# A two-layer graph network on one core: preparation steps divided, edge counts moved beside the keys, the phases left beside the same groups

## The chip, the cores and the metric

The kernel runs on one core of a Trainium2 chip. The metric is the device time of one execution in microseconds; the time before is the median of three runs. The profile is of one execution.

The engines are TensorE (PE in the profile, PEld for its weight loads), VectorE (DVE), ScalarE (ACT), GpSimd (POOL) and SyncE (SP), which issues the DMAs. Each runs its own queue in order; semaphores tie them together.

## The reference

For each of 32 graphs with 512 nodes and 128 features:

```python
# layer 0
adj = adj + eye(N);  degree = adj.sum(axis=2);  d = degree ** -0.5   (0 where infinite)
x = layernorm(x + (d[:, :, None] * adj * d[:, None, :]) @ (x @ weight) + bias)
# layer 1
pre = (x @ W1[:D])[:, None, :, :] + (x @ W1[D:])[:, :, None, :] + b1      # every pair (i, j)
msg = gelu(layernorm(pre) * g1 + be1)
agg = einsum('bijo,bij->bio', msg, adjacency)
updated = layernorm(concat([x, agg]) @ W2 + b2) * g2 + be2
out = layernorm(x + updated)
```

About one in sixteen of the entries of `adj` is not zero, and a message counts only where the entry isn't.

## The kernel before

The kernel makes messages for the edges alone. A graph's 512 nodes are C = 4 blocks of P = 128, so the adjacency is 16 blocks of 128 x 128. For each node and block, `lists` finds the first 8 edges (VectorE's max and index of a key that ranks them), `more` finds 16 more (match, replace, max, index: lines 455 to 458), and `shared` packs what is left over into 2 more slots per block. The first 8 slots, one slot for the diagonal blocks' ninth edge and the 2 shared ones make the list `order` of 41 groups a graph: 8 x 4 + 1 + 2 x 4.

The main loop runs over 32 graphs and their 41 groups. In the iteration of group k, counted within its graph:

- `pairs` (lines 724, 725, and 720 for the shared slots) issues TensorE's products of group k into one of 3 PSUM tiles;
- `pass_on` issues the aggregate (L772, TensorE) of group k-3, the sums (L734, VectorE, which release the PSUM tile) and the weights (L749, GpSimd, 4 buffers) of group k-1, and the messages (L763, ScalarE, four activations) of group k-2;
- `advance(todo)` runs one step of `finish`, the tail of the graph before: it starts in iteration 2 of the next graph;
- `prepare` runs steps of the preparation phases of graphs to come.

Ahead of both, `fetch` issues the index loads, the one-hot comparison (L687, VectorE), its transposing DMA and the row loads of the slots that begin 5 and 3 groups later.

A phase is a Python generator, and a step is what it issues up to its next `yield`. The list `plan` gives each phase a number of steps and a range of iterations, relative to the graph that it prepares. The steps are spread evenly:

```python
while gen[1] < n_steps * (g + 1 - n0) // (n1 - n0):
```

So a phase with more steps than iterations runs two of them in some iterations. With 41 groups a graph, `layer0` (range -41 to -19) lies beside the iterations 0 to 21 of the graph before, `lists` beside 22 to 32, `more` beside 31 to 40 of the graph before and 0 to 7 of its own, `shared` beside 8 to 27 of its own. Within an iteration the order is: `finish`, `layer0`, `lists`, `parts`, `factors`, `more`, `shared`.

The instructions of ScalarE, GpSimd and VectorE stay in the order in which Python issues them (`tc.manual_schedule`). TensorE's and SyncE's order is made by the framework's scheduler.

Names and lines that matter here, in `layer0`: `a_nat` (the adjacency as loaded), `pa` (its transposed blocks in PSUM, L249), `copied` with `deg` (L260, ScalarE, row sums), `a_t` (L261, ScalarE's copy out of PSUM), `mask` (L263, VectorE, one instruction over all four blocks), the chain of small GpSimd instructions from the degrees to `dinv` (lines 277 to 287), `xb` (L289, GpSimd), the edge counts (L293, ScalarE, four activations that sum rows of the mask), `s` and `own_s` (L297, L302, ScalarE), `xb` plus `own_s` (L306, GpSimd), `pconv` (L311, TensorE), `y` (L318, VectorE), the norm (statistics L194 and L196 on VectorE, `ve`, `rstd`, `shift` on GpSimd in lines 199, 187, 204, 205, result L208 on ScalarE), `x1t` (L328), `pat` and `pct` (L333, L335), and the keys (L361, L362 on VectorE after L365 on TensorE). In `shared`: `over`, `count`, `here`, `counts` (lines 469 to 479, VectorE), `last`, `most` and `missed` (L493 to L501), the places (L502, L505, GpSimd), `ended` (L512, sixteen VectorE comparisons), `pj` and `sj` (L526 TensorE, L522 VectorE, eight each), `pl` and `sent` (L537 TensorE, L533 ScalarE, sixteen each). In `finish`: `pu` (L637, L638, TensorE), `u` (L641, VectorE), two norms with three additions and products of GpSimd between them (lines 645 to 649). `bank` hands out 4 PSUM banks in turn; a new user of a bank waits for the readers of the one before.

Of the kernel before, what the change touches and what calls it, by code (L numbers as in the profile page):

```python
# [8 lines left out]
F32 = mybir.dt.float32  # L9
BF16 = mybir.dt.bfloat16  # L10
I32 = mybir.dt.int32
U32 = mybir.dt.uint32
AF = mybir.ActivationFunctionType
ALU = mybir.AluOpType
# [4 lines left out]
P = 128  # L19
# [8 lines left out]
def bcast(ap, n):  # L28

    return ap.unsqueeze(1).to_broadcast([ap.shape[0], n, ap.shape[-1]])  # L30
# [16 lines left out]
def sparse_path(ctx, tc, x, adj, w0, b0, w1, b1, g1, be1, w2, b2, g2, be2, out, most):  # L47
# [21 lines left out]
    nc = tc.nc  # L69
    B, N, D = x.shape  # L70
    C = N // P
# [3 lines left out]
    node = ctx.enter_context(tc.tile_pool(name="node", bufs=1))  # L75
    small = ctx.enter_context(tc.tile_pool(name="small", bufs=2))
# [66 lines left out]
    rows = {}  # L143
# [69 lines left out]
    def bank(key):  # L213
        return ps.tile([P, 512], F32, tag="ps", name=key)

    def transposed(src, key):

        pt = bank(f"pt_{key}")
        for c in range(C):
            nc.tensor.transpose(pt[:, c * P : (c + 1) * P], src[:, c, :], ident)  # L220
        return pt
# [3 lines left out]
    def pause(n):  # L225

        for _ in range(n):
            yield

    def layer0(b):  # L230

        st = state[b] = {}
        xs = node.tile([P, C, D], F32, tag="xs", name=f"xs_{b}")
# [5 lines left out]
        a_t = big.tile([P, C, C, WIDE], F32, tag="a_t", name=f"a_t_{b}", bufs=2)  # L239
        st["a_t"] = a_t  # L240
        edges = small.tile([P, C], F32, tag="edges", name=f"edges_{b}")
        st["edges"] = edges
        deg = small.tile([P, C], F32, tag="deg", name=f"deg_{b}")
        mask = big.tile([P, C, N], BF16, tag="mask", name=f"mask_{b}")
        px = transposed(xs, f"x_{b}")
        for mc in range(C):
            pt = bank(f"pa_{b}_{mc}")
            for c in range(C):
                nc.tensor.transpose(  # L249
                    pt[:, c * P : (c + 1) * P], a_nat[:, c, mc * P : (mc + 1) * P], ident  # L250
                )
            if mc == 2:
                psup = bank(f"psup_{b}")
                for c in range(C):
                    nc.tensor.matmul(
                        psup[:, c * P : (c + 1) * P], x_t[:, c * P : (c + 1) * P], w0_sb, start=True, stop=True
                    )
            yield
            copied = small.tile([P, N], BF16, tag="copied", name=f"copied_{b}_{mc}", bufs=1)
            nc.scalar.activation(copied, a_nat[:, mc, :], AF.Copy, accum_out=deg[:, mc : mc + 1])  # L260
            nc.scalar.copy(a_t[:, mc, :, :P], pt.rearrange("p (c i) -> p c i", i=P))  # L261
            if mc == C - 1:
                nc.vector.tensor_scalar(  # L263
                    mask.rearrange("p q (c i) -> p (q c) i", i=P),
                    a_t.rearrange("p q c w -> p (q c) w")[:, :, :P],
                    0.0,
                    1.0,
                    ALU.is_equal,
                    ALU.subtract,
                )  # L270
            if mc == 0:
                x_t = node.tile([P, N], F32, tag="t0", name=f"x_t_{b}")
                nc.scalar.copy(x_t, px)
        yield from pause(2)

        deg1 = small.tile([P, C], F32, tag="deg1", name=f"deg1_{b}")
        nc.gpsimd.tensor_scalar(deg1, deg, 1.0, None, ALU.add)
# [6 lines left out]
        dinv = small.tile([P, C], F32, tag="dinv", name=f"dinv_{b}")  # L284
        nc.gpsimd.tensor_sub(dinv, rdeg, none)
        dinv2 = small.tile([P, C], F32, tag="dinv2", name=f"dinv2_{b}", bufs=1)
        nc.gpsimd.tensor_tensor(dinv2, dinv, dinv, ALU.mult)
        xb = node.tile([P, C, D], F32, tag="t2", name=f"xb_{b}")
        nc.gpsimd.tensor_tensor(xb, xs, bcast(rows["b0"], C), ALU.add)  # L289

        for q in range(C):
            copied = small.tile([P, N], BF16, tag="copied", name=f"counted_{b}_{q}", bufs=1)
            nc.scalar.activation(copied, mask[:, q, :], AF.Copy, accum_out=edges[:, q : q + 1])  # L293

        s = node.tile([P, C, D], F32, tag="t1", name=f"s_{b}")
        for c in range(C):
# [10 lines left out]
        pt = bank(f"pconv_{b}")  # L307
        for c in range(C):
# [4 lines left out]
                )  # L313
            if c % 2:
                yield
        y = node.tile([P, C, D], F32, tag="t3", name=f"y_{b}")
        for c in range(C):
            nc.vector.scalar_tensor_tensor(  # L318
                y[:, c, :], pt[:, c * P : (c + 1) * P], dinv[:, c : c + 1], xb[:, c, :], ALU.mult, ALU.add
            )  # L320
        x1 = node.tile([P, C, D], F32, tag="x1", name=f"x1_{b}", bufs=3)
        yield from layernorm(y, x1, f"l0_{b}")
        st["x1"] = x1
# [1 line left out]
        pt = transposed(x1, f"x1_{b}")  # L325
# [31 lines left out]
        key = big.tile([P, C, N], F32, tag="key", name=f"key_{b}")  # L357
        for q in range(C + 1):
            if q:
                here = key[:, q - 1, :]  # L360
                nc.vector.scalar_tensor_tensor(here, pt, a_sum[:, q - 1 : q], c_sum, ALU.add, ALU.add)  # L361
                nc.vector.scalar_tensor_tensor(here, here, -TINY, mask[:, q - 1, :], ALU.min, ALU.mult)  # L362
            if q < C:
                pt = bank(f"pv_{b}_{q}")
                nc.tensor.matmul(pt, at2[:, q * P : (q + 1) * P], ct, start=True, stop=True)  # L365
            yield
# [94 lines left out]
    def shared(b):  # L461
# [7 lines left out]
        nc.vector.scalar_tensor_tensor(over, var, 0.0, sharing, ALU.is_gt, ALU.mult)  # L469
        count = small.tile([P, C * C], F32, tag="count", name=f"count_{b}", bufs=1)  # L470
        nc.vector.tensor_reduce(count, over, AX.X, ALU.add)

        here = small.tile([P, C * C, SLOTS], F32, tag="here", name=f"here_{b}", bufs=1)
        nc.vector.tensor_scalar(here, st["top"], 0.0, None, ALU.is_gt)
# [11 lines left out]
        pt = bank(f"po_{b}")  # L486
# [32 lines left out]
        pt = None  # L519
        for k in range(len(chunks) + 1):  # L520
            if k:
                nc.vector.tensor_scalar(sj_f[:, chunks[k - 1]], pt, node_p, None, ALU.is_equal)  # L522
            if k < len(chunks):
                pt = bank(f"pj_{b}_{k}")
# [6 lines left out]
        for n in range(C * C + 1):  # L531
            if n:
                nc.scalar.copy(sent[:, n - 1], pt[:, : SHARED * WIDE].rearrange("p (k w) -> p k w", w=WIDE))  # L533
            if n < C * C:
                pt = bank(f"pl_{b}_{n}")
                for k in range(SHARED):
                    nc.tensor.matmul(  # L537
                        pt[:, k * WIDE : (k + 1) * WIDE],
                        sj[:, n, k * P : (k + 1) * P],
                        at[:, n, :],  # L540
                        start=True,
                        stop=True,
                    )
            if n % 2:
                yield
        yield from pause(3)

        n_r = SHARED * C * C
        chosen = big.tile([P, 2, SHARED, C * C, MORE], F32, tag="mask", name=f"chosen_{b}")
# [22 lines left out]
        pt = bank(f"pidx_s_{b}")  # L572
# [18 lines left out]
        pt = bank(f"psd_s_{b}")  # L591
# [38 lines left out]
    def finish(b):  # L630

        st = state.pop(b)
        aggt = st["aggt"]
        pt = bank(f"pu_{b}")
        for c in range(C):
            o, here = pt[:, c * P : (c + 1) * P], slice(c * P, (c + 1) * P)
            nc.tensor.matmul(o, st["x1t"][:, here], w2_sb[:, 0, :], start=True, stop=False)  # L637
            nc.tensor.matmul(o, aggt[:, here], w2_sb[:, 1, :], start=False, stop=True)  # L638
        yield
        u = node.tile([P, C, D], F32, tag="f0", name=f"u_{b}")  # L640
        nc.vector.tensor_tensor(u, pt.rearrange("p (c d) -> p c d", d=D), bcast(rows["b2"], C), ALU.add)  # L641
        yield
        un = node.tile([P, C, D], F32, tag="f1", name=f"un_{b}")
        yield from layernorm(u, un, f"l1_{b}")
        nc.gpsimd.tensor_tensor(un, un, bcast(rows["g2"], C), ALU.mult)
        yield
        nc.gpsimd.tensor_tensor(un, un, bcast(rows["be2"], C), ALU.add)
        yield
        nc.gpsimd.tensor_tensor(un, un, st["x1"], ALU.add)
        yield  # L650
        o_sb = node.tile([P, C, D], F32, tag="f0", name=f"o_sb_{b}")
        yield from layernorm(un, o_sb, f"l2_{b}")
        yield
        nc.sync.dma_start(out[b].rearrange("(c p) d -> p c d", p=P), o_sb)
# [111 lines left out]
    def aggregate(b, t, q, m, sw):  # L766
        st = state[b]
        begin, end = (t, q) == order[0], (t, q) == order[-1]
        if begin:
            st["agg"] = ps_g.tile([P, C, P], F32, tag="agg", name=f"agg_{b}")  # L770
        for c in range(C):
            nc.tensor.matmul(  # L772
                st["agg"][:, c, :],
                m[:, c, :],
                sw[:, c, :],
                start=(begin and c == 0),
                stop=(end and c == C - 1),
            )
        if end:
            st["aggt"] = node.tile([P, N], F32, tag="f1", name=f"aggt_{b}")  # L780
            nc.scalar.copy(st["aggt"], st["agg"].rearrange("p c i -> p (c i)"))
            todo.append(finish(b))

    def advance(gens, steps=1):
# [12 lines left out]

    n_groups = len(order)
    plan = [
        (layer0, 26, -n_groups, -19),  # L800
        (lists, 21, -19, -8),
        (parts, 7, -19, -10),
        (factors, 7, -8, -3),
        (more, 33, -10, 8),
        (shared, 45, 8, 28),
    ]
    running = {}

# [260 lines left out]
def kernel(  # L1069
# [32 lines left out]
    with ExitStack() as inner:  # L1102
        sparse_path(inner, tc, *args, most)
# [42 lines left out]
```

## Time and profile before

| what | value |
|---|---|
| median of 3 runs | 4013.91 us (4012.98 to 4014.3) |
| profiled execution, its own time | 4011.64 us |
| its span, first to last instruction | 4009.9 us |
| mean granted TensorE clock | 0.985 |
| busy: TensorE, VectorE, ScalarE, GpSimd | 94%, 81%, 70%, 55% of the span |
| VectorE's whole mask (L263) | 32 x 1.218 us |
| ScalarE's counts (L293) | 128 x 0.626 us, and 128 x 0.186 us for reading the sums |
| VectorE's `ended` (L512) | 512 x 0.337 us |

A line of a group or of the timeline names the line of the kernel, the engine, the instruction, what it writes and reads, and the shapes; in the timeline the first two numbers are start and duration in us, and what stands in brackets is how long the engine stood idle before it and what ended that. Instructions of one engine overlap a little at their ends, so what one costs its queue is read from its start to the start of the next.

### The profile page before, as it was taken

To read this page: it belongs to the slowest core of one execution; us is meant where nothing else is said; L and a number is where in the kernel's file an instruction comes from. 1 tells how busy PE (TensorE), PEld (TensorE's weight loads), DVE (VectorE), ACT (ScalarE), POOL (GpSimd) and SP (SyncE) were. 2 spreads that over 40 slices of the span, in tenths; PEclk is the share of its full clock that TensorE was granted. 3 is DMA by queue.
4 is the path that set the end of the run, shared out by engine and by line. 5 is a ranking of instruction groups with operands and counts; after the bars stand their busy time and mean duration, and the time that the engine had idled before them with its cause. 6 is when DMAs were issued, how large, how long until landed. Compare 5 with 4: busy or idle time off the path is not lost. (4 is left out here: it accounts for less than half of the span.)

```text
span 4009.9 us, 108439 instructions
## 1 busy us (share of the span) xinstructions
PE 3766.3 (94%) x39744; PEld 3510.3 (88%) x39744; DVE 3263.9 (81%) x10645; ACT 2791.9 (70%) x8321; POOL 2225.5 (55%) x2526
## 2 busy tenths in 40 slices
PE   5999999999999999999999999999999999999997
PEld 5988889888899888898888998888998889888887
DVE  6888888888887888888888888888888888788892
ACT  4777677676776766776767767667767677676664
POOL 4555565555655555655556555556555565555554
PEclk7999999999999999999999999999999999999998
DMA  3444444444444444444444444444444444444442
GB/s 85 107 109 106 114 101 106 107 107 105 113 102 106 108 106 110 106 106 106 107 105 113 102 106 108 106 112 104 106 105 108 105 108 106 108 107 105 98 105 56
DMA packets 902107, 419.99 MB, mean 105 GB/s; under 512 B 724304, under 2 KB 882192, under 8 KB 901568
## 3 DMA queue, kind: packets, MB, share of 16 engines
q1 hardware_dynamic: 901344, 412.52, 44.1%
q8 instruction: 317, 5.19, 0.5%
q14 instruction: 222, 1.82, 0.1%
q0 software_dynamic: 224, 0.46, 0.1%
HBM read 227.15 MB, written 13.76 MB: 60 GB/s over the span
## 5 line engine op out<-in xcount | busy, mean ns | idle before, releaser
L749 POOL TENSOR_TENSOR sw<-mt,a_t 128x512 f32<-128x512 bf16 x1056 | 1216.8, 1164 | 918.1 <-PE agg L772 764.0
L772 PE MATMUL agg<-sw,m 128*128 128x128 f32 x10496 | 1495.7, 285 | 76.2 <-POOL sw L749 46.1
L724 PE MATMUL u<-c,s 128*128 128x128 bf16 x15744 | 1433.9, 220 | 84.0 <-DVE u_sb L734 80.3
L763 ACT ACTIVATE m<-u_sb,r 128x128 f32<-128x128 f32 x4096 | 1294.0, 395 | 142.3 <-DVE u_sb L734 57.8
L772 PEld LDWEIGHTS agg<-sw,m 128*128 128x128 f32 x10496 | 1304.5, 192 | 94.2 <-POOL sw L749 51.3
L724 PEld LDWEIGHTS <-s 128*128 128x128 bf16 x15744 | 1191.2, 98 | 115.0 <-issue 40.9
L725 PE MATMUL u<-be,sd_rows 128*128 128x128 bf16 x5248 | 1148.6, 220 | 20.7 <-DMA sd_rows<-sd_ds 14.6
L734 DVE TENSOR_TENSOR u_sb<-u,ac 128x512 f32<-128x512 f32 x1056 | 713.4, 676 | 200.6 <-PE u L725 177.1
L725 PEld LDWEIGHTS <-sd_rows 128*128 128x128 bf16 x5248 | 512.7, 98 | 30.7 <-issue 20.0
L763 ACT ACTIVATE m<-u,r_s 128x128 f32<-128x128 f32 x1024 | 288.3, 363 | 251.6 <-PE agg L772 247.4
L533 ACT COPY sent<-pl 128x352 f32<-128x352 f32 x512 | 228.9, 447 | 315.9 <-PE pl L537 278.8
L687 DVE TENSOR_SCALAR s<-raw,node_p 128x2052 bf16<-128x2052 bf16 (+1 forms) x352 | 421.5, 1197 | 20.6 <-DMA raw<-idx_ds 11.9
L720 PE MATMUL u<-ac,sj 128*128 128x128 f32 x2048 | 437.8, 296 | 0.0
L749 POOL TENSOR_TENSOR sw<-mt,sent 128x512 f32<-128x512 bf16 x256 | 296.4, 1163 | 229.0 <-PE agg L772 176.2
L537 PEld LDWEIGHTS pl<-a_t,sj 128*128 128x128 f32 x2048 | 316.2, 191 | 60.7 <-issue 59.2
L457 DVE MAX8 a_t<-key 128x8 f32<-128x128 f32 x1024 | 301.2, 294 | 34.5
L537 PE MATMUL pl<-a_t,sj 128*128 128x176 f32 x2048 | 327.4, 313 | 1.3 <-POOL a_t L505 1.3
L522 DVE TENSOR_SCALAR sj<-pj,node_p 128x512 f32<-128x512 f32 x256 | 187.7, 745 | 153.8 <-PE pj L526 153.8
L720 PEld LDWEIGHTS u<-ac,sj 128*128 128x128 f32 x2048 | 310.0, 192 | 0.4
L458 DVE FIND_INDEX8 idx_m<-a_t,key 128x8 uint32<-128x128 f32 x1024 | 291.4, 285 | 0.0
L311 PEld LDWEIGHTS pconv<-s,a_t 128*128 128x128 f32 x1024 | 141.3, 214 | 57.1 <-ACT s L297 55.4
L361 DVE SCALAR_TENSOR_TENSOR key<-pv,a_sum,c_sum 128x512 f32<-128x512 f32 x128 | 95.7, 748 | 108.3 <-PE pv L365 108.3
(178 smaller groups left out, 4788.8 us busy)
## 6 DMA issues: line engine op xcount, KB each, us to landing
raw<-idx_d SPq DMA_DIRECT2D x256, 513.0 KB
raw<-idx_ds SPq DMA_DIRECT2D x64, 513.0 KB
a_nat<-in_adj_dram SPq DMA_DIRECT2D x32, 1024.0 KB
sd_rows<-sd_d SPq DMA_DIRECT2D x768, 12.0 KB
xs<-in_x_dram SPq DMA_DIRECT2D x32, 256.0 KB
out_dram<-o_sb SPq DMA_DIRECT2D x32, 256.0 KB
mt<-s SPq DMA_TRANSPOSE x352
raw<-idx_ds SPq DMA_DIRECT2D x32, 129.0 KB
```

The source lines that it names most:

```text
L457: nc.vector.max(found, k)
L458: nc.vector.max_index(idx[:, n, h : h + 8], found, k)
L533: nc.scalar.copy(sent[:, n - 1], pt[:, : SHARED * WIDE].rearrange("p (k w) -> p k w", w=WIDE))
L537: nc.tensor.matmul(pt[:, k * WIDE : (k + 1) * WIDE], sj[:, n, k * P : (k + 1) * P], at[:, n, :], start=True, stop=True,)
L687: nc.vector.tensor_scalar(s.rearrange("p (k e) -> p k e", k=3), raw, node_p, None, ALU.is_equal)
L720: nc.tensor.matmul(pu[:, c, :], place, state[b]["ac"][:, q, 0, :], start=first, stop=False)
L724: nc.tensor.matmul(pu[:, c, :], here, c3[:, k, c, :], start=(first and k == 0), stop=False)
L725: nc.tensor.matmul(pu[:, c, :], dev[:, q, c, :], be9, start=False, stop=(c == C - 1))
L734: nc.vector.tensor_tensor(u, pu, a if t == EXTRA else bcast(a[:, q, :], C), ALU.add)
L749: nc.gpsimd.tensor_tensor(sw, mt[:, 0] if t == EXTRA else mt[:, :, q, :], a, ALU.mult)
L763: nc.scalar.activation(m[:, c, :], u[:, c, :], AF.Gelu, scale=r[:, k : k + 1])
L772: nc.tensor.matmul(st["agg"][:, c, :], m[:, c, :], sw[:, c, :], start=(begin and c == 0), stop=(end and c == C - 1),)
```

## The change

No product, sum or copy is added or dropped but that the mask is made by four instructions, one per block of rows, instead of one. What changes is in which step, and so in which iteration and place of the queue, an instruction is issued:

- the quarters of the mask are made one step after the copy that they read; the last one, with `xb`, has a step of its own;
- the degrees' chain on GpSimd and the scaling by it on ScalarE are in steps of their own;
- the four edge counts are issued beside the four keys;
- `y` is made in two halves, each a step after its half of `pconv`, and the norm's statistics a step after that;
- in `shared`, the first step is cut in two, and each of the sixteen products `pl` has a step of its own;
- in `finish`, one iteration is left out after the product with `g2` and one after the addition of `be2`;
- the plan has 28 steps for `layer0` (26 before) and 54 for `shared` (45 before), over the same ranges.

```diff
--- before.py
+++ after.py
@@ -242,6 +242,12 @@
         st["edges"] = edges
         deg = small.tile([P, C], F32, tag="deg", name=f"deg_{b}")
         mask = big.tile([P, C, N], BF16, tag="mask", name=f"mask_{b}")
+
+        def masked(q):
+            nc.vector.tensor_scalar(
+                mask[:, q, :].rearrange("p (c i) -> p c i", i=P), a_t[:, q, :, :P], 0.0, 1.0, ALU.is_equal, ALU.subtract
+            )
+
         px = transposed(xs, f"x_{b}")
         for mc in range(C):
             pt = bank(f"pa_{b}_{mc}")
@@ -259,19 +265,16 @@
             copied = small.tile([P, N], BF16, tag="copied", name=f"copied_{b}_{mc}", bufs=1)
             nc.scalar.activation(copied, a_nat[:, mc, :], AF.Copy, accum_out=deg[:, mc : mc + 1])
             nc.scalar.copy(a_t[:, mc, :, :P], pt.rearrange("p (c i) -> p c i", i=P))
-            if mc == C - 1:
-                nc.vector.tensor_scalar(
-                    mask.rearrange("p q (c i) -> p (q c) i", i=P),
-                    a_t.rearrange("p q c w -> p (q c) w")[:, :, :P],
-                    0.0,
-                    1.0,
-                    ALU.is_equal,
-                    ALU.subtract,
-                )
+            if mc:
+                masked(mc - 1)
             if mc == 0:
                 x_t = node.tile([P, N], F32, tag="t0", name=f"x_t_{b}")
                 nc.scalar.copy(x_t, px)
-        yield from pause(2)
+        yield
+        masked(C - 1)
+        xb = node.tile([P, C, D], F32, tag="t2", name=f"xb_{b}")
+        nc.gpsimd.tensor_tensor(xb, xs, bcast(rows["b0"], C), ALU.add)
+        yield
 
         deg1 = small.tile([P, C], F32, tag="deg1", name=f"deg1_{b}")
         nc.gpsimd.tensor_scalar(deg1, deg, 1.0, None, ALU.add)
@@ -285,12 +288,7 @@
         nc.gpsimd.tensor_sub(dinv, rdeg, none)
         dinv2 = small.tile([P, C], F32, tag="dinv2", name=f"dinv2_{b}", bufs=1)
         nc.gpsimd.tensor_tensor(dinv2, dinv, dinv, ALU.mult)
-        xb = node.tile([P, C, D], F32, tag="t2", name=f"xb_{b}")
-        nc.gpsimd.tensor_tensor(xb, xs, bcast(rows["b0"], C), ALU.add)
-
-        for q in range(C):
-            copied = small.tile([P, N], BF16, tag="copied", name=f"counted_{b}_{q}", bufs=1)
-            nc.scalar.activation(copied, mask[:, q, :], AF.Copy, accum_out=edges[:, q : q + 1])
+        yield
 
         s = node.tile([P, C, D], F32, tag="t1", name=f"s_{b}")
         for c in range(C):
@@ -313,11 +311,13 @@
                 )
             if c % 2:
                 yield
-        y = node.tile([P, C, D], F32, tag="t3", name=f"y_{b}")
-        for c in range(C):
-            nc.vector.scalar_tensor_tensor(
-                y[:, c, :], pt[:, c * P : (c + 1) * P], dinv[:, c : c + 1], xb[:, c, :], ALU.mult, ALU.add
-            )
+                if c == 1:
+                    y = node.tile([P, C, D], F32, tag="t3", name=f"y_{b}")
+                for k in (c - 1, c):
+                    nc.vector.scalar_tensor_tensor(
+                        y[:, k, :], pt[:, k * P : (k + 1) * P], dinv[:, k : k + 1], xb[:, k, :], ALU.mult, ALU.add
+                    )
+        yield
         x1 = node.tile([P, C, D], F32, tag="x1", name=f"x1_{b}", bufs=3)
         yield from layernorm(y, x1, f"l0_{b}")
         st["x1"] = x1
@@ -357,6 +357,9 @@
         key = big.tile([P, C, N], F32, tag="key", name=f"key_{b}")
         for q in range(C + 1):
             if q:
+
+                copied = small.tile([P, N], BF16, tag="copied", name=f"counted_{b}_{q}", bufs=1)
+                nc.scalar.activation(copied, mask[:, q - 1, :], AF.Copy, accum_out=edges[:, q - 1 : q])
                 here = key[:, q - 1, :]
                 nc.vector.scalar_tensor_tensor(here, pt, a_sum[:, q - 1 : q], c_sum, ALU.add, ALU.add)
                 nc.vector.scalar_tensor_tensor(here, here, -TINY, mask[:, q - 1, :], ALU.min, ALU.mult)
@@ -469,6 +472,7 @@
         nc.vector.scalar_tensor_tensor(over, var, 0.0, sharing, ALU.is_gt, ALU.mult)
         count = small.tile([P, C * C], F32, tag="count", name=f"count_{b}", bufs=1)
         nc.vector.tensor_reduce(count, over, AX.X, ALU.add)
+        yield
 
         here = small.tile([P, C * C, SLOTS], F32, tag="here", name=f"here_{b}", bufs=1)
         nc.vector.tensor_scalar(here, st["top"], 0.0, None, ALU.is_gt)
@@ -541,9 +545,8 @@
                         start=True,
                         stop=True,
                     )
-            if n % 2:
-                yield
-        yield from pause(3)
+            yield
+        yield from pause(2)
 
         n_r = SHARED * C * C
         chosen = big.tile([P, 2, SHARED, C * C, MORE], F32, tag="mask", name=f"chosen_{b}")
@@ -643,9 +646,9 @@
         un = node.tile([P, C, D], F32, tag="f1", name=f"un_{b}")
         yield from layernorm(u, un, f"l1_{b}")
         nc.gpsimd.tensor_tensor(un, un, bcast(rows["g2"], C), ALU.mult)
-        yield
+        yield from pause(2)
         nc.gpsimd.tensor_tensor(un, un, bcast(rows["be2"], C), ALU.add)
-        yield
+        yield from pause(2)
         nc.gpsimd.tensor_tensor(un, un, st["x1"], ALU.add)
         yield
         o_sb = node.tile([P, C, D], F32, tag="f0", name=f"o_sb_{b}")
@@ -797,12 +800,12 @@
 
     n_groups = len(order)
     plan = [
-        (layer0, 26, -n_groups, -19),
+        (layer0, 28, -n_groups, -19),
         (lists, 21, -19, -8),
         (parts, 7, -19, -10),
         (factors, 7, -8, -3),
         (more, 33, -10, 8),
-        (shared, 45, 8, 28),
+        (shared, 54, 8, 28),
     ]
     running = {}
```

## The prediction

> **What bounds the kernel now.** I read first the page's busy shares, then the list of waits, then one batch of 32 in the timeline, engine by engine.
>
> ```profile
> PE 3766.3 (94%) x39744; PEld 3510.3 (88%) x39744; DVE 3263.9 (81%) x10645; ACT 2791.9 (70%) x8321; POOL 2225.5 (55%) x2526
> ```
>
> TensorE is busy nearly always, so the change can only win the time in which it waits. The list of waits (engine and line, what for, us in total, times, longest):
>
> ```profile
> POOL ve_l L199 <- DVE mv_l L196: 163.1, 66, 8.5
> ...
> DVE u L641 <- PE pu L638: 89.0, 32, 27.6
> PE u L724 <- DVE u_sb L734: 80.3, 69, 2.2
> ...
> PE agg L772 <- POOL sw L749: 46.1, 30, 1.6
> ...
> PE agg L772 <- ACT m L763: 30.0, 20, 1.5
> ...
> PE pidx L408 <- ACT idx_h L404: 15.4, 15, 5.1
> ```
>
> The matrix engine waits for all three others, about once a batch each. Where in the batch? Number the groups of a batch, and the loop's iterations with them, 0 to 40. The sums of group k are made in iteration k+1, its messages in k+2, its aggregate in k+3; the products of group k+3 need the PSUM tile that the sums of k release. Two stretches of the batch that I follow (busy us by engine, granted clock, DMA), the first from iteration 3 to 13:
>
> ```profile
> core 0: us, PE busy (x) PEld busy (x) DVE busy (x) ACT busy (x) POOL busy (x), PEclk, DMA share, GB/s
> 2033.10:2063.80 30.70, 28.36 (x314) 27.56 (x311) 29.98 (x110) 24.99 (x80) 23.37 (x34) 0.94 0.38 82
> ...
> 2072.60:2098.00 25.40, 25.40 (x218) 22.46 (x216) 14.77 (x22) 14.02 (x41) 5.82 (x5) 1.00 0.46 127
> ```
>
> In the second, TensorE runs without a gap and nothing else matters. In the first, VectorE is full: 29.98 of 30.70 us, the rest being the seams between instructions. What is added to VectorE there, or makes it wait, comes out as time; what is taken from ScalarE or moved on GpSimd helps only if VectorE lets it. Its own timeline, with the lines of the others that I use:
>
> ```profile
> 2032.42 0.69 DVE L641 TENSOR_TENSOR u<-pu,b_row 128x512 f32<-128x512 f32 x1 [2.05 <-PE pu L638]
> 2033.03 0.08 DVE L455 MATCH_VALUE_LOAD key<-a_t,key 128x8 f32 x1
> ...
> 2040.36 1.22 DVE L263 TENSOR_SCALAR mask<-a_t 128x2048 bf16<-128x2048 f32 x1
> 2041.49 0.08 DVE L455 MATCH_VALUE_LOAD key<-a_t,key 128x8 f32 x1
> ...
> 2063.14 0.68 DVE L734 TENSOR_TENSOR u_sb<-u,ac 128x512 f32<-128x512 f32 x1
> ```
> ```profile
> 2034.92 0.57 ACT L261 COPY a_t<-pa 128x512 f32<-128x512 f32 x1
> ```
> ```profile
> 2057.53 0.23 POOL L199 TENSOR_SCALAR ve_l<-mv_l 128x4 f32<-128x4 f32 x1 [3.39 <-DVE mv_l L196]
> ```
> ```profile
> 2065.97 1.16 PE L772 MATMUL agg<-sw,m 128*128 128x128 f32 x8 [1.55 <-POOL sw L749]
> ```
>
> The first line is the last idle time of VectorE (iteration 3, the older batch's tail); the sums at 2063.14 are group 12's (iteration 13). GpSimd stood idle 3.39 us in iteration 10 for the norm's statistics, with the weights of group 10 queued behind; after the chains and group 11's weights, the aggregate of group 11 started at 2065.97. From there TensorE is behind no one (group 12 at 2068.29, group 13 at 2072.67). So two paths meet: VectorE's queue, and the statistics plus GpSimd's chain.
>
> **The change part by part.** Layer 0 now has 28 steps over the same 22 iterations; after iteration d, 28(d+1)/22 rounded down are done, so two steps fall together in iterations 3, 7, 10, 14, 18 and 21.
>
> *Mask in quarters.* The steps that fall together in iteration 3 hold ScalarE's copies of the second and third transposed blocks, and on VectorE quarters 0 and 1 of the mask, ahead of the list search (L455 to L458). Quarter 1 reads the copy that ends at 2034.92 + 0.57 = 2035.49, and ScalarE is full ahead of it. VectorE comes to it at 2033.03 + 0.33 and stands for 2.1 us. A quarter: the whole takes 1.13 us to the next start (2040.36 to 2041.49), so 0.28 if it divides evenly, and up to 0.83, what the four-column tensor_scalar of L479 takes beside a GpSimd multiply; I take 0.33, near even division. The search starts at 2035.49 + 0.06 + 0.33 = 2035.88: +2.85 us. Quarters 2 and 3 for the whole: 2 x 0.33 - 1.13 = -0.47. Quarter 3 falls in a stretch where GpSimd is full: 0 to 0.83 - 0.06 of waiting; I take 0.5.
>
> The row for that: L479 takes 0.83 us for 4 columns while a reduction of 12 (L497) takes 0.16, and each time it ends as the GpSimd instruction beside it ends. The Trainium skill (SBUF — State Buffer, Who interferes with whom) says that a VectorE tensor_scalar in a two-port mode and a GpSimd instruction exclude each other for the whole instruction; that rule speaks against cutting one mask into four claims. By the page alone each quarter could wait a whole GpSimd instruction.
>
> *Counts (L293).* 4 x (0.63 + 0.19), 2.97 us of ScalarE between 2043.20 and 2046.17, leave iteration 6 for iterations 18 to 21, where ScalarE has room (14.02 of 25.40 us). TensorE's waits at 2044 to 2050 mostly go; VectorE had no gap there, so by itself this ends nothing sooner. If ScalarE were full in 18 to 21, it would cost the same 2.97.
>
> *Layer 0's `y`, `xb`, and the norm.* The addition to `xb` (1.27 us of GpSimd) moves one iteration up, `y` is halved over two, and GpSimd's chain and ScalarE's `x` each come one iteration after what they wait for: the 3.39 us wait no longer holds group 10's weights. VectorE's sum is unchanged.
>
> *Tail of the older batch.* Its last statistics (1.06 us of VectorE) move from iteration 10 to 12, its GpSimd chain to 13, its last four activations (L208, 1.64 us) to 14. VectorE's total to group 12 is unchanged.
>
> *Shared lists.* 54 steps for 45 put twelve threshold pieces (L512) into iteration 12 where eight were: 4 x 0.255 = +1.02 us ahead of group 12's sums. Two `pj` products (0.43 us of TensorE) come earlier into its idle time. The `sent` copies are spread; TensorE was full there: nothing. Six list products instead of four come after the last key product, 2 x 0.6 us more of TensorE before the wait for `idx_h` (15.4/32 = 0.48 us a batch): 0 to -0.48, I take -0.3.
>
> *Sum for a batch.* VectorE to group 12's sums: 2.85 - 0.47 + 0.5 + 1.02 = +3.9, so they end at 2067.7 instead of 2063.8. Products of group 15 (0.89) follow, then the aggregate of group 12: 2068.6 to 2068.7 instead of 2068.29, +0.4. GpSimd's path: statistics at 2057.43 + 2.85 - 0.47 + 0.5 - 1.06 = 2059.3, plus its chain 2.0, missed and places 2.1, weights 1.2: 2064.6, early enough. Next ScalarE in iteration 14: messages of group 12 (1.28), the tail's activations (1.64), `x1t` (0.57): 2067.7 + 3.5 = 2071.2, where L333 had started at 2069.24. TensorE could stand idle from 2069.6 to 2071.3. If it keeps program order, the end of group 13's aggregate with all `pj` done is 1.65 late (idle 1.75 and 0.4, less 0.43 of `pj`, less rounding); if the order puts 0.89 of products and 0.43 of `pj` into the gap, 0.3. TensorE's order isn't written by hand and is not to be seen here; in this trace it mixes `pj` into products, so I take the middle, +1.0. With -0.3: **+0.7 us a batch**. Over the 31 batches that have this stretch: +22 us. Once, the preparation before the first group loses the counts from its chain: -2 us.
>
> The profiled execution took 4011.64 us (span 4009.9), 2.3 below the median of 4013.91. 4011.6 + 22 - 2 = 4032; on the median's footing **4034 us**.
>
> **Rivals.** *Faster: GpSimd's wait sets the end.* If quarter 1 doesn't hold VectorE (the copy is there when VectorE comes to it), VectorE is late by 3.9 - 2.1 = 1.8, group 12 is ready at 2066.6, 1.7 before now, less what `x1t` takes back (0 to 0.6), with -0.3: -1.4 a batch, 31 x -1.4 - 2 = -45: 3969 us. For it: 163.1 us of GpSimd waits and 76 us of TensorE waits behind ScalarE and GpSimd. Against: ScalarE has no gap before 2035.49. It decides as soon as VectorE's wait in iteration 3 is under 1.4 us.
>
> *Clearly slower: TensorE's order.* `pj` products 3 and 4 take the PSUM banks that the first two `sj` comparisons release, now in the same iteration; if group 15's products stay behind them (0.7 us each) and `x1t` too, a batch loses 2 to 3 us: 4076 to 4107.
>
> *Nothing:* the in-order wait is filled wholly (+0.3 - 0.3), 4012.
>
> **How the numbers follow.** Forecast 0.46 (4022 to 4060), faster 0.32, clearly slower 0.13, nothing 0.09. No change is within 0.2% (8 us), about what a measurement of this kernel can tell. Faster 0.32, same 0.10, slower 0.58. The range takes in the faster case (3969, and 3950 with quarters of 0.28 that never wait) and the clearly slower one: 3950 to 4107.
>
> **What would show it.** Right: a new wait of VectorE for ScalarE's `a_t` copy, 2 us, 31 times; no counts at iteration 6; GpSimd's wait for the statistics under 100 us; TensorE's wait for `u_sb` over 80 us and for weights near 0. Wrong: no such VectorE wait, or group 12's aggregate, measured from the end of L641, under 34 us (35.1 now).

## The result and the profile after

| | before | after |
|---|---|---|
| median of 4 runs each | 4013.69 us (4012.98 to 4014.3) | 4210.79 us (4206.76 to 4212.33) |
| ratio, 95% interval | | 1.049 [1.0471, 1.0508] |
| profiled execution, span | 4011.64, 4009.9 us | 4206.76, 4205.1 us |
| mean granted clock | 0.985 | 0.976 |

The change costs 197 us. 31 graphs have the stretch that the prediction followed, so this is 6.4 us a graph (the prediction's batch) where 0.7 were forecast: the sign was right, the size was not.

Lines moved by three: L644 is what was L641, L737 was L734, L775 was L772. First the page's busy shares:

```profile
PE 3843.8 (91%) x39744; PEld 3553.6 (85%) x39744; DVE 3256.0 (77%) x10741; ACT 2762.8 (66%) x8321; POOL 2207.8 (53%) x2526
```

VectorE has 96 instructions more (three more pieces of mask for each of 32 graphs) and is busy 8 us less. No engine got more to do. Of the 195 us by which the span grew, TensorE stands idle 118 (361 us instead of 244); the other 77.5 are a longer busy time for the same 39744 matmuls, at a mean granted clock of 0.976 instead of 0.985. The list of waits of the kernel after (engine and line, what for, us in total, times, longest):

```profile
POOL ve_l L199 <- DVE mv_l L196: 140.4, 34, 8.8
...
PE u L727 <- DVE u_sb L737: 126.2, 93, 2.2
POOL ve_l L199 <- DVE last L497: 118.9, 31, 5.1
...
DVE s L690 <- DMA raw<-idx_ds: 97.9, 33, 4.4
...
DVE y L317 <- PE pconv L309: 83.0, 33, 4.7
PE pconv L309 <- DVE y L317: 77.3, 32, 2.7
...
DVE mask L247 <- ACT a_t L267: 67.4, 31, 4.9
...
PE pidx L411 <- ACT idx_h L407: 47.9, 34, 5.1
...
PE psd L435 <- ACT sd L426: 28.2, 32, 2.4
```

Three families are new or much longer, each about once a graph. VectorE waits for the copy `a_t`. TensorE waits for `y` and VectorE for `pconv`, in turn, which was in no list before. At the end of `shared`, VectorE waits for the load of rows (11.9 us before), TensorE for `idx_h` (15.4 before) and for `sd` (2.4 before).

The stretch from the end of L644 to the end of group 12's sums, the same one that took 30.70 us before:

```profile
core 0: us, PE busy (x) PEld busy (x) DVE busy (x) ACT busy (x) POOL busy (x), PEclk, DMA share, GB/s
2007.20:2043.50 36.30, 31.54 (x331) 30.23 (x329) 31.41 (x116) 22.25 (x73) 25.88 (x38) 0.91 0.27 70
```

VectorE comes 5.60 us later to its end: 1.43 are work (31.41 against 29.98) and 4.17 are idle. Its timeline names the 4.17. The first half is the mask:

```profile
2007.09 0.42 DVE L247 TENSOR_SCALAR mask<-a_t 128x512 bf16<-128x512 f32 x1
2009.59 0.43 DVE L247 TENSOR_SCALAR mask<-a_t 128x512 bf16<-128x512 f32 x1 [2.08 <-ACT a_t L267]
2009.94 0.08 DVE L458 MATCH_VALUE_LOAD key<-a_t,key 128x8 f32 x1
```

The other half is `y` (all engines, in the same graph):

```profile
2029.98 0.59 DVE L317 SCALAR_TENSOR_TENSOR y<-pconv,dinv,xb 128x128 f32<-128x128 f32 x2
...
2030.63 2.67 PE L309 MATMUL pconv<-s,a_t 128*128 128x128 f32 x16 [2.52 <-DVE y L317]
2033.34 0.61 DVE L317 SCALAR_TENSOR_TENSOR y<-pconv,dinv,xb 128x128 f32<-128x128 f32 x2 [2.09 <-PE pconv L309]
```

TensorE has stood idle 2.52 us when VectorE has read the first two blocks of `pconv`; only then does it write the other two, and for that VectorE stands idle 2.09 us. The two engines take turns on one PSUM tile: 2.08 + 2.09 is the 4.17. Over the 31 graphs the stretch has a median of 36.90 us, against 30.65 before.

### The profile page after: what moved, and what is told of

Read it like the earlier page. It is cut to its first block, busy times and chain, and to the rows that moved or that the text cites. A ratio compares the mean times of both kernels' runs of the same rounds, so it can differ in the third digit from the quotient of the medians.

```text
span 4205.1 us, 108201 instructions
## 1 busy us (share of the span) xinstructions
PE 3843.8 (91%) x39744; PEld 3553.6 (85%) x39744; DVE 3256.0 (77%) x10741; ACT 2762.8 (66%) x8321; POOL 2207.8 (53%) x2526
## 5 line engine op out<-in xcount | busy, mean ns | idle before, releaser
L727 PE MATMUL u<-c,s 128*128 128x128 bf16 x15744 | 1428.5, 220 | 130.5 <-DVE u_sb L737 126.2
L775 PE MATMUL agg<-sw,m 128*128 128x128 f32 x10496 | 1510.3, 287 | 14.4 <-ACT m L766 13.1
L775 PEld LDWEIGHTS agg<-sw,m 128*128 128x128 f32 x10496 | 1320.2, 194 | 34.2 <-issue 23.7
L737 DVE TENSOR_TENSOR u_sb<-u,ac 128x512 f32<-128x512 f32 x1056 | 712.1, 677 | 119.6 <-PE u L728 101.2
L541 PE MATMUL pl<-a_t,sj 128*128 128x176 f32 x2048 | 349.4, 314 | 1.1 <-POOL a_t L509 1.1
L309 PE MATMUL pconv<-s,a_t 128*128 128x128 f32 x1024 | 162.1, 325 | 81.5 <-DVE y L317 77.3
L309 PEld LDWEIGHTS pconv<-s,a_t 128*128 128x128 f32 x1024 | 151.5, 235 | 88.0 <-DVE y L317 83.4
```

The lines of the kernel that those rows point to most:

```text
L309: nc.tensor.matmul(o, a_t[:, mc, c, :P], s[:, mc, :], start=(mc == 0), stop=(mc == C - 1))
L541: nc.tensor.matmul(pt[:, k * WIDE : (k + 1) * WIDE], sj[:, n, k * P : (k + 1) * P], at[:, n, :], start=True, stop=True,)
L727: nc.tensor.matmul(pu[:, c, :], here, c3[:, k, c, :], start=(first and k == 0), stop=False)
L737: nc.vector.tensor_tensor(u, pu, a if t == EXTRA else bcast(a[:, q, :], C), ALU.add)
L775: nc.tensor.matmul(st["agg"][:, c, :], m[:, c, :], sw[:, c, :], start=(begin and c == 0), stop=(end and c == C - 1),)
```

## The experiments

Each kernel is compared with the kernel before on the same chip; a ratio has its 95% interval. Differences between ratios are turned into us with 4011.

**Three parts of the change, one taken away at a time.** The first leaves `y` in one step, after both halves of `pconv`:

```diff
-                if c == 1: y = ...
-                for k in (c - 1, c):
-                    nc.vector.scalar_tensor_tensor(y[:, k, :], ...)
+        for k in range(C):                      # after the loop over c
+            nc.vector.scalar_tensor_tensor(y[:, k, :], ...)
```

> The changed kernel, with y made in one step after both halves of pconv (steps and everything else as in the change). Theory A (the two halves of pconv share one PSUM tile, so TensorE's second half waits until VectorE has read the first, and VectorE then waits for the second half: 2.6 us of VectorE a graph, 31 graphs): 4211 - 80 = about 4130 us, and the waits of pconv for y and of y for pconv gone. Theory B (the loss is what the prediction named, VectorE's wait in iteration 3 and the fuller queue; the halves cost nothing): 4211 within 10 us.

Measured: 1.0350 [1.0333, 1.0367], 4149.26 us. The second keeps the halves and gives each its own bank:

```diff
-        pt = bank(f"pconv_{b}")
         for c in range(C):
+            if c % 2 == 0:
+                pt = bank(f"pconv_{b}_{c}")
```

> The changed kernel, y still in halves at the same steps, but each half of pconv in a PSUM bank of its own. Theory A (the shared tile makes the wait): as good as y in one step, 4120 to 4140 us. Rival (the halves' place in VectorE's queue makes the loss, not the tile): 4211 within 10 us, or worse by the extra bank.

Measured: 1.0338 [1.0320, 1.0355], 4147.42 us. The turns are gone from both lists: with two banks VectorE waits for `pconv` twice in the whole run (5.3 us) and TensorE never for `y`, and with one step a single wait is left:

```profile
DVE y L316 <- PE pconv L309: 8.7, 1, 8.7
```

Two edits with nothing in common but that VectorE no longer reads a tile of which TensorE has still to write the other half save the same 0.014 to 0.015, some 56 to 61 us. So it is the shared tile that costs, not the halves. The granted clock rose with them: its mean over a run lies between 0.972 and 0.977 in the four runs each of the change and of the two kernels below that keep the turns, and between 0.981 and 0.988 with `y` in one step or on two banks. No run shows why, or what the clock alone is worth. In the few graphs whose clock was 1.00 throughout, a graph took 128.00 us with the turns (median of 3) and 126.38 with `y` in one step (19), so most of the gain is there without it.

The third moves two empty steps of `shared` from behind the `sent` copies to its end, so that the shared slots' indices and rows are issued earlier:

```diff
-        yield from pause(2)          # after the loop over pl and sent
...
-        yield                        # the last one of shared
+        yield from pause(3)
```

> The changed kernel, with the two empty steps after the sent copies moved to the end of the phase, so that the index rows of the shared slots are written and their deviations made in the iterations of the kernel before. Theory A (the index rows reach memory too late for the load that is issued in iteration 27; VectorE stands for it 2.5 to 3 us a graph, and the lists behind it make TensorE wait): 31 x 2.0 to 2.4 us less, about 4140 us, and VectorE's wait for that load (97.9 us) under 20. Theory B (that wait only takes the place of others): 4211 within 10 us.

Measured: 1.0348 [1.0331, 1.0365], 4148.62 us, 57 us better than the change. Its waits:

```profile
PE pidx L411 <- ACT idx_h L407: 18.4, 33, 5.1
...
DVE s L689 <- DMA raw<-idx_ds: 9.7, 11, 3.7
```

Both are near their values of before. The timelines say how. After, SyncE's queue (SPq) and VectorE:

```profile
1957.86 0.85 SPq L389 DMA_DIRECT2D idx_ds<-idx_rs  x1
...
1960.36 0.92 SPq L680 DMA_DIRECT2D raw<-idx_ds  x2
...
1965.63 0.48 DVE L690 TENSOR_SCALAR s<-raw,node_p 128x516 bf16<-128x516 bf16 x1 [2.50 <-DMA raw<-idx_ds]
```

And the same three in the kernel before:

```profile
1981.53 0.27 SPq L386 DMA_DIRECT2D idx_ds<-idx_rs  x1
...
1987.20 1.26 SPq L677 DMA_DIRECT2D raw<-idx_ds  x2
...
1992.22 0.48 DVE L687 TENSOR_SCALAR s<-raw,node_p 128x516 bf16<-128x516 bf16 x1
```

The load of the shared slots follows the write of their indices by 5.7 us before and by 2.5 us after. From the load's issue to the comparison it is 5.0 and 5.3 us; before, the rows were there when VectorE came to the comparison; after, VectorE stood 2.50 us for them. The index write is late, and the load behind it.

The fourth gives each mask quarter one step more after its copy:

```diff
-            if mc:
-                masked(mc - 1)
+            if mc > 1:
+                masked(mc - 2)
...
+        masked(C - 2)
         masked(C - 1)
```

> The changed kernel, with each quarter of the mask two steps after its copy instead of one (the last two together), so that VectorE meets finished copies. Theory A and B both (VectorE's queue sets the end of the stretch): 2.1 us a graph less, about 4146 us, and VectorE's wait for the a_t copy (67.4 us) gone. Rival (the later wait of VectorE for the second half of pconv swallows it): 4211 within 15 us.

Measured: 1.0377 [1.0358, 1.0396], 4159.01 us, 45 us better. The wait for `a_t` is no longer among the long ones (67.4 us before the edit), but the turns on `pconv` grew from 77.3 and 83.0 us:

```profile
PE pconv L310 <- DVE y L318: 97.5, 32, 3.2
...
DVE y L318 <- PE pconv L310: 90.7, 33, 5.0
```

So the wait that is taken away comes back in part at the next one, as the expectation's rival had it, but only in part: 45 of 67 us are saved.

**The three together, and then the tail too.**

> The changed kernel with three repairs together: y in one step, the two empty steps of the shared phase at its end, each mask quarter two steps after its copy. Theory A (three separate losses at three places): the gains add up, 1.049 - 0.014 - 0.014 - 0.011 = 1.0095 of before, about 4050 us. Theory B (one queue, each repair only shifts the same wait): no more than the best one, 4149. What is then left over before is the clump of twelve threshold pieces and the tail's activations ahead of x1t: 0 to 1 us a graph.

Measured: 1.0046 [1.0029, 1.0062], 4027.87 us. The three save 0.0444, 178 us, where one at a time they save 158; the intervals of the five ratios leave the difference open by about 20 us, so they add up, as theory A had it, and no more is shown. The next takes back the two pauses in `finish` as well (`yield from pause(2)` to `yield`, twice):

> The kernel with three repairs, and the tail of the older graph without its two empty iterations, as in the kernel before. If the tail's four activations ahead of x1t cost what the prediction gave them (0 to 1.3 us a graph): 0 to 40 us less than with three repairs. Rival (its statistics now fall on layer 0's, and GpSimd's chain is later): 0 to 30 us more.

Measured: 0.9990 [0.9980, 1.0000], 4007.65 us: 0.0056, 22 us or 0.7 us a graph, for the pauses. What is left of the change now neither wins nor loses: counts, chains apart, quarters, and `shared` in 54 steps.

**Parts of the change put into the kernel before.** The counts alone:

```diff
-        for q in range(C):                      # in layer0
-            nc.scalar.activation(copied, mask[:, q, :], AF.Copy, accum_out=edges[:, q : q + 1])
...
+                nc.scalar.activation(copied, mask[:, q - 1, :], ...)   # in each key's step
```

> The kernel before, with nothing changed but the edge counts, which are issued beside the keys. Prediction's reading (VectorE has no gap in that stretch, so 2.97 us less of ScalarE end nothing sooner): within 0.3% of before, 4002 to 4026 us, with TensorE's waits at that place moved. Rival (ScalarE's block of counts sets the time there): 31 x up to 2.97 us less, down to 3920 us.

Measured: 1.0025 [1.0015, 1.0035], 4021.09 us. TensorE's waits for `u_sb` and for weights fall, from 80.3 and 46.1 us, and the waits for messages rise from 30.0; the aggregate of group 11 does not start sooner (32.83 us after the end of what was L641, 32.80 before; these times are medians of the 31 graphs, here and below):

```profile
PE agg L770 <- ACT m L761: 76.8, 31, 2.5
...
PE u L722 <- DVE u_sb L732: 50.2, 69, 2.2
...
PE agg L770 <- POOL sw L747: 16.5, 16, 1.6
```

The next has the counts beside the keys and `layer0` in the change's 28 steps, with three exceptions: the mask stays whole, one step after the last copy, and `y` stays whole; `shared` and `finish` are as before.

> The kernel before, with the counts beside the keys and layer 0 in 28 steps: the degrees' chain, the scaling, y in one step, the statistics and the norm each in a step of their own; the mask whole, one step later; the shared phase and the older graph's tail as before. Theory A (VectorE's work in the stretch is as before and GpSimd's 3.4 us wait for the statistics no longer holds the weights): VectorE sums group 12 at the old time and its aggregate need not wait, 2 to 3.4 us a graph less, 3910 to 3952 us. Rival (the stretch is VectorE's anyway, or another wait comes up): 4000 to 4025 us.

Measured: 0.9841 [0.9825, 0.9858], 3945.91 us. The same stretch of its profile, from the end of L642 (which was L641) to group 12's sums (columns as above):

```profile
1882.90:1913.60 30.70, 27.21 (x325) 26.50 (x322) 29.98 (x110) 23.86 (x77) 26.49 (x37) 1.00 0.37 91
```

VectorE takes the same 30.70 us with the same 29.98 busy as before; and yet group 12's aggregate starts 32.67 us after L642's end instead of 35.12, and group 11's at 29.79 instead of 32.80. GpSimd's wait for the statistics fell from 163.1 to 61.4 us, and TensorE's wait for the weights, 46.1 us before, to one:

```profile
POOL ve_l L199 <- DVE mv_l L196: 61.4, 40, 8.5
...
PE agg L773 <- POOL sw L750: 1.2, 1, 1.2
```

This is the mechanism of the prediction's faster rival: with VectorE untouched, GpSimd's queue did set the end. The clock is not what made the difference: among the graphs whose granted clock was 1.00 throughout, a graph took 122.36 us before (median of 19) and 119.97 here (24). Which of the steps set apart counts for how much was not separated.

**Added to that kernel, one at a time.** First `shared` in 54 steps, with its empty steps at the end:

> The kernel with layer 0's steps apart, and the shared phase in 54 steps with its two empty steps at the end. The kernel with four repairs differs from the one with the steps apart in this and in the mask's quarters, and is 62 us slower. Theory A (twelve threshold pieces in one iteration delay VectorE's sums, as the prediction had it with 1.02 us a graph, and more by the statistics beside them): 30 to 62 us slower than with the steps apart, 3976 to 4008 us. Rival (the quarters' claims on the port that VectorE and GpSimd share make the difference): 3946 within 10 us.

Measured: 0.9999 [0.9989, 1.0008], 4009.6 us: 0.0158, 64 us or 2.0 a graph. VectorE's timeline ahead of the sums of group 12:

```profile
1940.09 3.13 DVE L514 TENSOR_SCALAR ended<-places,last 128x258 bf16<-128x258 bf16 x12
1943.14 1.26 DVE L687 TENSOR_SCALAR s<-raw,node_p 128x2052 bf16<-128x2052 bf16 x1
1944.33 0.67 DVE L734 TENSOR_TENSOR u_sb<-u,ac 128x512 f32<-128x512 f32 x1
```

Twelve pieces stand there where eight did (2.12 us), and the sums end 31.75 us after L641's end instead of 30.71: +1.04. Group 12's aggregate is 1.56 later (34.23). The rest of the 2.0 was not separated.

Then the mask in quarters, each two steps after its copy:

> The kernel with layer 0's steps apart, and the mask in quarters, each two steps after its copy. Theory A (a quarter costs VectorE about 0.33 us and waits little): 0 to 15 us slower than with the steps apart, 3946 to 3961 us. Rival (each quarter waits for GpSimd, 4 x 0.5 us a graph): about 62 us slower, 4008 us.

Measured: 0.9832 [0.9815, 0.9849], 3945.0 us, the same as without. Cutting the mask costs nothing that these intervals can tell; where a quarter stands does. Then one empty iteration in the tail, after the addition of `be2`:

> The kernel with layer 0's steps apart, and one empty iteration in the older graph's tail, so that its last four activations fall in iteration 13, between layer 0's norm (12) and x1t (14), instead of beside the norm. TensorE's wait for messages at group 11 (51.8 us in 30 times) comes from both in iteration 12: 31 x up to 1.6 us less, 3896 to 3946 us. Rival (VectorE's sums are late there too, or the later statistics delay them): 3946 within 10 us, or slower.

Measured: 0.9860 [0.9844, 0.9877], 3956.15 us. It is 0.0019 above the kernel without it and the intervals overlap, so this one run does not settle what a pause costs; the pair above (22 us for both) does. Theory A's gain did not come: TensorE's wait for messages fell from 51.8 to 31.0 us, but its wait for weights rose from 1.2 to 22.7.

**A version that beats both.** In the kernel with the chains apart, the mask's quarters are made at the keys, each just ahead of the key that needs it; in the trace two of them fall in iteration 18 and one each in 19 and 20 (the expectation says 17 to 20):

```diff
-        nc.vector.tensor_scalar(mask ...)       # the whole mask, after the last copy
...
+                masked(q)
                 pt = bank(f"pv_{b}_{q}")
```

> The kernel with layer 0's steps apart, and the mask taken out of the stretch in which VectorE is full: its quarters are made in iterations 17 to 20, each a step before the key and the count that read it. Theory A (VectorE's sum of work in iterations 3 to 13 sets that stretch's time): 1.13 us a graph less, 31 x 1.13 = 35 us, about 3910 us. Rival (with GpSimd's wait gone, ScalarE's messages or TensorE set the end there): 3945 within 10 us.

Measured: 0.9774 [0.9758, 0.9790], 3919.7 us, 2.3% faster than before. The mask leaves the stretch in which VectorE is full, group 12's sums end 29.74 us after L641's end, and TensorE's wait for `u_sb` is less than half of the 63.7 us of the kernel with the chains apart:

```profile
PE u L724 <- DVE u_sb L734: 30.3, 62, 2.2
```

## Why the prediction was wrong in its size

The account, in us against the kernel before. Each row is the step from one kernel of the chain to the next, so the sum must close; what the runs show is how the 197 us divide:

| part | us |
|---|---|
| `layer0`'s chains in steps of their own, counts beside the keys (0.9841) | -64 |
| `shared` in 54 steps, with the empty ones at its end (0.9999) | +64 |
| mask in quarters, away from their copies (0.9990 against 0.9999, intervals overlap) | -4 |
| pauses in `finish` (1.0046 against 0.9990) | +22 |
| `y` in halves, a mask quarter right after its copy, `shared`'s index rows late, together (1.049 against 1.0046) | +178 |
| sum | +196 |
| measured | +197 |

- **The failed step: `y`.** "`y` is halved over two ... VectorE's sum is unchanged" priced the edit by its instructions, and those did not change. The edit puts a read of the tile between two writes of it. That adds two waits, 77.3 us of TensorE and 83.0 of VectorE in all, and 56 to 61 us in the time. Nothing in the trace of before shows such a pair, since there all of `pconv` comes first. The diff does show it: one `bank` ahead of the loop, and now a reader within it.
- **The second failed step: `shared`'s tail.** "The `sent` copies are spread; TensorE was full there: nothing", and -0.3 us for the wait on `idx_h`. The sign was wrong. I looked at where the copies went and not at what they pushed: the index write and the load behind it, which the shared slots need at a fixed group. VectorE stands for that load, and what it does next is late for TensorE's `pidx` and `psd` (47.9 and 28.2 us of waiting, 18.4 and 2.4 with the index write early again). It costs 57 us, 1.8 a graph. Counting every DMA of a moved step would have led there.
- **The mask: right.** VectorE was to stand 2.1 us, 31 times: 67.4 / 31 = 2.17. The search was to start 2.85 us later: 2009.94 - 2007.09 = 2.85. The quarters are busy 69.0 us in all where the whole mask took 32 x 1.218 = 39.0, 0.94 us a graph more, and 0.69 was forecast. The rule of the Trainium skill (SBUF — State Buffer, Who interferes with whom) that VectorE in a two-port mode and GpSimd lock each other out, the one that comes second waiting for the other, agrees with the rows. Begun while GpSimd's weights still ran, the whole mask took a median of 1.858 us (chains apart), and the last quarter 0.78 in the graph read of the change; begun as one GpSimd instruction ended and ahead of the next, the whole took 1.218 (before) and that next one, `degp`, 1.15 instead of the 0.20 that it takes in the change; a quarter with none beside it took 0.42. What the prediction read out of the rule did not come: four claims in place of one cost nothing (0.9832 against 0.9841).
- **What I made of the 2.85: too little.** The sum had VectorE 3.9 us late and the aggregate of group 12 only 0.4. VectorE was 5.60 late, and by the same steps that would be 2.1; in the same two graphs group 12's aggregate started 38.33 us after L644's end instead of 35.18, 3.2 late (in the median of 31 graphs 38.97 and 35.12). The sum had only group 15's products, 0.89 us, between the sums and that aggregate. In the trace `pj` stands between them too and waits for VectorE, so that it is 2.03 (the lines follow). And taking the wait for `a_t` away saved 45 us by itself.

```profile
2044.18 0.38 PE L530 MATMUL pj<-ended,ones_h 128*128 128x512 bf16 x1 [0.44 <-DVE sj L526]
...
2045.50 1.11 PE L775 MATMUL agg<-sw,m 128*128 128x128 f32 x8
```

- **`ended`: right in its place, too small in all.** +1.02 was forecast, +1.04 came; the whole division of `shared` costs 2.0 us a graph.
- **Pauses in the tail: right in size.** I took 1.0 us a graph for ScalarE's activations ahead of `x1t`, between 0.3 and 1.65; the two pauses cost 0.7. That it is these activations was not shown.
- **Counts: right** that they end nothing sooner; they cost 10 us.
- **The faster rival** was a true mechanism (-64 us), worth more than the -45 given. Its condition was too narrow: with VectorE's wait in iteration 3 gone and the other repairs made too, the kernel takes 4007.65 us and not 3969, since `shared` in 54 steps (+64) covers the gain as well.
- **The clearly slower rival** (4076 to 4107) came nearest, by luck. The order that it names is there: TensorE stands before `pj` for `sj` 32 times, with products of group 15 behind it. But that is 14.3 us in all (0.2 before), not 62 to 93.
- **The signs that I gave.** The wait for `a_t` is there; TensorE's wait for `u_sb` is over 80 us, at 126.2. TensorE's wait for weights is near 0, at 0.3 us. GpSimd's wait for the statistics was to fall under 100 us and rose from 163.1 to 259: 140.4, and 118.9 that the profile puts down to `last`, the VectorE instruction right behind layer 0's statistics. In the graph read that is 3.37 us, as long as the 3.39 of before; what went is its hold on the weights.

## What to carry to other kernels

When a step is cut, list for each half the tiles that it shares with the other: a reader placed between two writers of one tile made both engines wait here, though no instruction count told of it, and a second bank removed it. When steps are inserted, follow the last thing the phase issues, the index write or the load, to whoever needs it at a fixed time. Take work out of the stretch where the bounding engine is full (the mask at the keys, 27 us) before cutting it finer there, which won nothing (0.9832 against 0.9841).

## What the hardware showed that I had not expected

- A write to DRAM and the load of the same data: in the graph shown the load went out 2.5 us after the write, and the comparison started 5.3 us after that, with VectorE waiting 2.50.
- The clock granted in the stretch differs from graph to graph within one trace. Before, where VectorE is full, the stretch is as long with a lower clock: 30.60 us at 1.00 in the graph below and 30.70 at 0.94 in the one that the prediction shows, with TensorE busy 26.73 and 28.36. In the kernel after, it is 35.70 at 1.00 (the graph that begins at 2135.70) and 36.30 at 0.91 (the graph shown above).

```profile
1788.80:1819.40 30.60, 26.73 (x313) 25.98 (x311) 29.88 (x108) 24.84 (x80) 23.35 (x34) 1.00 0.34 83
```
- The mask holds up GpSimd as well: its first instruction on `deg`, of four columns, took 0.23 us with no mask beside it (before), 0.40 beside a quarter (the change) and 1.20 beside the whole mask (chains apart).
